# Gating an attention by a feed-forward network on one core: sums gathered earlier, q kept once in DRAM and read in two halves, some pieces moved between engines

## The chip, the core and the metric

The kernel runs on one core of a Trainium2 chip. The core has five engines that each follow their own instruction stream: TensorE (PE in the profile, its weight loads PEld), VectorE (DVE), ScalarE (ACT), GpSimd (POOL) and SyncE (SP), which here does nothing but issue DMAs. Each engine works through its stream in order and waits on semaphores for the others. DMAs are moved by 16 DMA engines that all queues share.

The metric is the device time of one execution in microseconds (us). The time before is the median of three runs; the profile is one execution of its own.

## The reference, cut to what matters

The input has 8 sequences of 512 positions and 256 features. Each is normalised, goes through an attention with 16 heads of 16 features (rotary positions, a causal window of 250) and, beside it, through three layers whose weights are plus or minus one; the second gates the first.

```python
xn = _layernorm(x)
proj = xn @ in_proj_w.T                      # q, k, v of 16 heads x 16
q, k = _apply_rope(q, k)                     # rotates the pairs of features
mask = (delta >= 0) & (delta < 250)          # delta = row - column
scores = where(mask, q @ k.T * 16 ** -0.5, lowest)
s = (softmax(scores) @ v) @ out_proj_w.T
h = relu(s0 * (concat(xn, -xn) @ sign(k0))) * 2    # 512 -> 1024
h = relu(s1 * (h @ sign(k1))) * 2                  # 1024 -> 1024
g = silu(s2 * (h @ sign(k2)))                      # 1024 -> 256
out = x + s * g
```

All arrays are float32 and the signs are booleans.

## The kernel before

**Number format.** [...] an operand is split into a high and a low part, and the products of the parts are added. For the scores this is done by stacking: a head has 8 pairs of features, and for each pair k is laid on partitions as high, low, high, low and q as high, low, low, high, so that one product over 64 partitions adds all four combinations. Two heads fill the 128 partitions of a tile. These *stacks* are made by going through DRAM: `to_dram` (L514) writes the split k and q of one sequence into a DRAM tile, each part twice, at the places that the order above asks for, and `stack` (L538) reads them back, 256 KB contiguous in DRAM to 128 partitions of 2 KB. A group g is four heads, so a group needs two stacks of k and two of q ("pair" 0 and 1), and a sequence has four groups.

**One sequence.** `prepare` normalises it in a transposed form. `stats` takes the moments on DVE, with a power on POOL (L278). `lay_down` (L302) writes them to DRAM, and `lay_over` (L311) reads them back as `of_all`, every partition getting all 512 means and factors. `norm_turned` applies them to `xT` on DVE (L322), and `sum_x` (L341, POOL) makes sums of its quarters, from which `project_seven` (L461) projects k and q with seven products in place of eight, for sequences 2 to 7; its counterpart sums of the weights are made once by `sum_weights` (L177 and L178, POOL). Sequence 1 uses `project` (L413). DVE multiplies the projections by the rotation's tables (L434, L498), `rotate` adds them up on POOL (L512), `split_hi` copies the high part on ACT (L528, tiles `kh` and `qh`, which share one buffer), and `split_lo` subtracts on DVE (L535, in place in `m_ka` and `m_qa`). Each split is followed by its writes to DRAM (L521).

**Attention.** The scores (L850) are taken in six steps of three blocks a sequence, two groups to three steps: groups 0 and 1 in steps 0 to 2, groups 2 and 3 in steps 3 to 5. ACT takes exponentials (L875), POOL masks them (L895, L902), and the products with v (L932) follow a step later. `v_columns` holds columns of ones, so the same product gives each row's sum. When a group is done, `keep` takes values V and sums S out of PSUM: for even groups on ACT (L956, L957), for odd ones on DVE (L950, L951). S has two buffers.

**Row sums.** For every two groups ("pair" of `divisions`), `gather` (L1022) writes four rows of each S to DRAM, `pack` (L1030) reads them back spread over 128 partitions, `invert` takes reciprocals on DVE (L1036) and writes them (L1038), `unpack` (L1049) reads them as rows, and `divide` spreads these over the partitions (L1055, DVE) and multiplies V (L1056, POOL).

**Gate.** `last` (L666) makes the third layer, `scale` (L704) takes it out of PSUM. `gate_ready` (L729) takes the exponential and adds one on ACT (L731, L732), takes two reciprocals of half a tile each on DVE (L737), and multiplies on POOL (L739). `project_o` (L1066) projects the attention, `product` and `store` multiply, add the residual (`xr`, L649) and write out (L1088, L1095, L1096).

**Order.** The order on every engine is written out by hand. Each piece of work has a planned time on PE's own scale, in which a sequence takes `SEQ = 42.0` (its feed-forward layers alone), and `run` sorts all pieces by it. A piece may return follow-ups with a delay against the clock of costs added so far. Only the order that results matters on the chip; the waits are by semaphores. `attention` places the six steps at the pieces' times nearest to equal shares of the work, and places the reads of the stacks. While sequence b goes through its layers, the next one's moments, projections and first stack are made, and the output of the one before is finished.

Of the kernel before, what the change touches and what calls it, by code (L numbers as in the profile page):

```python
# [11 lines left out]
F32 = mybir.dt.float32  # L12
# [4 lines left out]
ALU = mybir.AluOpType  # L17
# [17 lines left out]
def tile_attention_times_gated_ffn(  # L35
# [42 lines left out]
    nc = tc.nc  # L78
    P = 128
    B, T, E = x.shape  # L80
    H = HEADS
    D = E // H
# [38 lines left out]
    first_half, second_half = s_sb[:, 3:4], s_sb[:, 4:5]  # L121
# [112 lines left out]
    SEQ = 42.0  # L234
# [168 lines left out]
    def project(b, what, part, half=None):  # L403

        st = states[b]
        col = E * "qk".index(what) + P * "ab".index(part)
        if half == 1:
            ps = st.pop(part)
        else:
            ps = st[part] = bank(f"{what}{part}_ps_{b}")  # L410
        for cols in [slice(0, T)] if half is None else [ts(half, T // 2)]:
            for c in range(EC):
                nc.tensor.matmul(  # L413
                    ps[:, cols], wqkv_sb[:, c, ds(col, P)], st["xT"][:, c, cols],
                    start=(c == 0), stop=(c == EC - 1),
                )
        if half == 0:
            return

        m = turned.tile(  # L420
            [P, 2, T], F32, tag=f"m{part}", name=f"m_{what}{part}_{b}",
            bufs=2,
        )
        st[what, part] = m

        hi_after, lo_after = (4.0, 5.1) if b else (5.0, 6.2) if what == "k" else (4.6, 5.4)
        both_done = [
            (1.4, lambda: rotate(b, what)),
            (hi_after, lambda: split_hi(b, what)),
            (lo_after, lambda: split_lo(b, what)),  # L430
        ]

        def times(i):
            nc.vector.tensor_tensor(  # L434
                m[:, i], ps, rope_sb[:, i if part == "a" else 1 - i], ALU.mult
            )

        def both():
            times(0)
            times(1)  # L440
            if part == "b":
                return both_done

        return [(1.5 if b == 0 and what + part == "qb" else 0.0, both)]
# [69 lines left out]
    def to_dram(b, what, part, tile_):  # L514

        st = states[b]
        if part == 0:
            st["dram", what] = dram.tile([P, 8, T], F32, tag=what, name=f"d{what}_{b}")
        for turn in range(2):
            place = 2 * turn + (part ^ (turn if what == "q" else 0))  # L520
            nc.sync.dma_start(  # L521
                st["dram", what][:, ds(2 * place, 2), :], tile_.bitcast(F32)
            )

    def split_hi(b, what):
# [12 lines left out]
    def stack(b, g):  # L538
        st = states[b]
        for pair in range(2):  # L540
            for what in "kq":
                t = stacks.tile([P, T], F32R, tag=f"{what}{pair}", name=f"{what}_{b}_{g}_{pair}")
                rows = st["dram", what][ds(32 * g + 16 * pair, 16)]
                nc.sync.dma_start(t.bitcast(F32), rows.rearrange("p n t -> (p n) t"))  # L544
                st[what, g, pair] = t

    def prepare(b, plain=False):
# [205 lines left out]
    def late(b, u):  # L753

        if b + 1 == B:
            return last_at(b, 3) + L3 + 0.9 * u
        return SEQ * (b + 1) + (33.5 + 4.9 * u if b + 2 < B else 19.2 + 5.0 * u)

    def finish_ffn(b, u, how):
        quick.add(last_at(b, u))  # L760
        out = [(last_at(b, u), L3 * (2 if b + 1 < B else 1), lambda: last(b, u, how))]
        if how == "later":
            out += [
                (late(b, u) - (6.6 if b + 2 < B else 4.6), 0, lambda: gate_ready(b, u)),
                (late(b, u) - 4.2, 0, lambda: residual(b, u)),
            ]
        return out
# [175 lines left out]
    def keep(b, g, po):  # L943

        st = states[b]
        odd = g % 2
        S = st["S", g] = outs.tile([P, T], F32, tag="S", name=f"S_{b}_{g}", bufs=2)
        if odd:
            V = st["V", g // 2]
            nc.vector.scalar_tensor_tensor(V, po, second_half, V, ALU.mult, ALU.add)  # L950
            nc.vector.tensor_copy(S, po)  # L951
        else:
            V = st["V", g // 2] = outs.tile(
                [P, T], F32, tag=f"V{g // 2}", name=f"V_{b}_{g}", bufs=2
            )
            nc.scalar.mul(V, po, first_half)  # L956
            nc.scalar.copy(S, po)  # L957

    def flush():
        if pending:  # L960
# [12 lines left out]
    def attention(b, among):  # L973

        first, end = SEQ * b + (24.7 if b == 0 else 0.0), ends_at(b)
        inside = sorted((at, cost) for at, cost, _ in among if first <= at < end)
        whole = sum(cost for _, cost in inside)
        times, done = [], 0.0
        places = {}
        for at, cost in inside:  # L980
            if at in quick or b == 0 and at not in inner:
                places[at] = done
            done += cost
        for n in range(len(steps)):
            at = min(places, key=lambda at: abs(places[at] * len(steps) - whole * n))
            del places[at]
            times.append(at - 0.01)
        out = []
        for n in range(len(steps)):
            out.append((times[n], 2.5, lambda n=n: step(b, n)))  # L990
        for g in range(NG):

            at = times[used[g - 2][-1]] + 0.01 if g > 1 else first - (
                7.6 if b == 0 else 4.0 if b == 1 else 9.0
            )
            if b and g == 3:
                at += 5.0
            if b and g == 1:
                at = first + 0.01
            out.append((at, 0, lambda g=g: stack(b, g)))  # L1000
        if b + 1 == B:
            out.append((end, 0.7, flush))
        return out
# [105 lines left out]
    def divisions(b, pairs=(0, 1)):  # L1109
        out = []  # L1110
        for pair in pairs:
            if b + 1 < B:
                first = SEQ * b + (30.0 if b else 38.4) if pair == 0 else SEQ * (b + 1) + 3.0
            else:
                first = SEQ * b + (22.5 if pair == 0 else 33.4)
            pieces = (gather, pack, invert, unpack, divide)
            very_last = b + 1 == B and pair == 1
            for f, at in zip(
                pieces,
                (0.0, 2.0, 4.4, 6.4, 9.0) if very_last  # L1120
                else (0.0, 2.4, 5.2, 7.6, 14.0 if pair and b + 2 < B else 10.6),
            ):
                out.append((first + at, 0, lambda p=pair, f=f: f(b, p)))
        return out
# [17 lines left out]
    def swap():  # L1142
# [5 lines left out]
        (-34.6, 0, signs), (-40.5, 0, lambda: warm(9)), (-34.7, 0, lambda: warm(0)),  # L1148
        (-31.0, 0, lambda: enough(0)),
        (-32.7, 0, lambda: first_parts(2, 3)),  # L1150
        (19.2, 0, make_w2), (22.5, 0, swap), (27.0, 0, sum_weights), (SEQ * (B - 1) + 47.6, 0, add_up),
        (SEQ * (B - 1) + 44.0, 0, hint),
    ]
    for c in range(EC):
# [153 lines left out]
```

## Time and profile before

| | |
|---|---|
| median of 3 runs | 634.32 us (632.41 to 639.65) |
| the profiled execution, its time | 632.67 us |
| its span, first to last instruction | 630.9 us |
| busy: PE, PEld | 598.9, 387.4 us |
| busy: DVE, ACT, POOL | 364.7, 314.9, 306.4 us |
| mean granted clock of PE | 0.983 |
| DMA | 92.27 MB in all; HBM read 53.22 MB, written 38.30 MB |
| q stacks read (L544) | 64 DMAs of 256 KB |
| q written (L521) | 32 DMAs of 512 KB |

A line of the groups or of a timeline gives a start or a count, a busy time, the engine, the line of the kernel, the operation and "out<-in" with the shapes; what stands in brackets is the engine's idle time just before and the instruction that ended it. A line of waits reads: who waited, for whom, us in total, how many times, the longest. For SP the duration is that of the issue, not of the transfer. A row of windows gives, for a stretch of time, its length, the busy time of each engine with its number of instructions, the granted clock, the mean busy share of the 16 DMA engines, and the rate in GB/s.

### The profile page before, as it was taken

To read this page: it belongs to the slowest core of one execution; us is meant where nothing else is said; L and a number is where in the kernel's file an instruction comes from. 1 tells how busy PE (TensorE), PEld (TensorE's weight loads), DVE (VectorE), ACT (ScalarE), POOL (GpSimd) and SP (SyncE) were. 2 spreads that over 40 slices of the span, in tenths; PEclk is the share of its full clock that TensorE was granted. 3 is DMA by queue.
4 is the path that set the end of the run, shared out by engine and by line. 5 is a ranking of instruction groups with operands and counts; after the bars stand their busy time and mean duration, and the time that the engine had idled before them with its cause. 6 is when DMAs were issued, how large, how long until landed. Compare 5 with 4: busy or idle time off the path is not lost.

```text
span 630.9 us, 10724 instructions
## 1 busy us (share of the span) xinstructions
PE 598.9 (95%) x3860; PEld 387.4 (61%) x3860; DVE 364.7 (58%) x638; ACT 314.9 (50%) x607; POOL 306.4 (49%) x502
## 2 busy tenths in 40 slices
PE   7998989999799998999989998999989999899996
PEld 6653656675566655566555764656646675567785
DVE  6835415676446864559634686357943679335346
ACT  4646554544446554454545445364545546465521
POOL 2737532647426473265533664344744456445513
PEclk9998989999899998999989999899999999999999
DMA  8663754207633076331753218441364505632101
GB/s 273 264 220 119 262 157 130 102 1 286 216 107 102 27 264 216 104 102 68 274 166 103 101 77 296 136 134 69 132 256 144 179 2 222 220 101 86 53 25 54
DMA packets 50089, 92.27 MB, mean 146 GB/s; under 512 B 10992, under 2 KB 18672, under 8 KB 50032
## 3 DMA queue, kind: packets, MB, share of 16 engines
q1 hardware_dynamic: 47600, 89.31, 41.4%
q10 hardware_dynamic: 2432, 2.23, 1.2%
q8 instruction: 32, 0.52, 0.3%
q14 instruction: 25, 0.20, 0.1%
HBM read 53.22 MB, written 38.30 MB: 145 GB/s over the span
## 4 chain that ended last, share of the span: by engine, by line
PE 63%; DVE 13%; DMA 9%; SPq 4%; POOL 4%; ACT 3%; issue 3%; POOLq 0%; ACTq 0%; DVEq 0%
PE h_ps L614 28%; PE po L932 9%; PE z_ps L666 9%; PE sc L850 5%; DMA q<-dq 5%; PE v_ps L393 4%; DMA dsums<-S 3%; PE k_ps L461 3%; DVE m_qa L498 2%; SPq L521 2%; DVE den L737 2%; PE q_ps L461 1%; DVE m_qa L535 1%; SPq L544 1%; DVE m_kb L498 1%
## 5 line engine op out<-in xcount | busy, mean ns | idle before, releaser
L875 ACT ACTIVATE p<-sc 128x512 f32<-128x512 f32 (+2 forms) x288 | 150.7, 601 | 69.5 <-PE sc L850 46.4
L895 POOL TENSOR_SCALAR_AFFINE_SELECT p<-p 128x256 f32<-128x256 f32 (+1 forms) x224 | 103.1, 471 | 105.5 <-ACT p L875 83.3
L614 PE MATMUL h_ps<-h1l,w_sb 128*128 128x512 f32 (+1 forms) x576 | 143.4, 391 | 0.0
L614 PE MATMUL h_ps<-h1h,w_sb 128*128 128x512 f16 (+1 forms) x576 | 124.2, 359 | 0.0
L614 PEld LDWEIGHTS h_ps<-h1l,w_sb 128*128 128x128 f32 x576 | 101.0, 189 | 22.6 <-issue 0.3
L614 PEld LDWEIGHTS <-w_sb 128*128 128x128 f16 x704 | 61.5, 98 | 85.2 <-issue 39.9
L625 ACT ACTIVATE h2h<-h_ps 128x512 f16<-128x512 f32 (+1 forms) x72 | 39.7, 552 | 99.8 <-PE h_ps L614 99.8
L932 PE MATMUL po<-p,v_pad 128*32 128x378 f32 (+4 forms) x1152 | 78.3, 406 | 1.9 <-POOL p L902 1.9
L850 PE MATMUL sc<-q,k 64*128 64x378 f32 (+4 forms) x576 | 59.7, 318 | 20.8 <-DMA q<-dq 14.6
L623 DVE SCALAR_TENSOR_TENSOR h2l<-h_ps,h2h 128x512 fp32r<-128x512 f32 (+1 forms) x72 | 44.6, 620 | 52.0 <-ACT h2h L625 52.0
L850 PEld LDWEIGHTS sc<-q,k 64*128 64x128 f32 x576 | 45.7, 189 | 45.2 <-issue 19.5
L623 DVE SCALAR_TENSOR_TENSOR h1l<-h_ps,h1h 128x512 fp32r<-128x512 f32 x64 | 43.0, 686 | 44.6 <-ACT h1h L625 44.6
L902 POOL TENSOR_SCALAR_AFFINE_SELECT p<-p 128x256 f32<-128x256 f32 x144 | 63.1, 438 | 0.3 <-POOL p L895 0.3
L625 ACT ACTIVATE h1h<-h_ps 128x512 f16<-128x512 f32 x64 | 37.6, 602 | 32.5 <-PE h_ps L614 32.5
L614 PE MATMUL h_ps<-xl,w_sb 128*128 128x512 f32 x128 | 52.8, 493 | 0.0
L737 DVE RECIPROCAL den<-den 128x256 f32<-128x256 f32 (+1 forms) x32 | 51.6, 1629 | 0.8 <-ACT den L732 0.8
L1095 POOL TENSOR_TENSOR gate<-gate,xr 128x512 f32<-128x512 f32 (+1 forms) x15 | 18.7, 1248 | 64.2 <-DVE gate L1088 36.3
L932 PEld LDWEIGHTS po<-p,v_pad 128*32 128x32 f32 x1152 | 33.3, 116 | 26.4 <-issue 15.5
L512 POOL TENSOR_TENSOR m_ka<-m_ka,m_kb 128x512 f32<-128x512 f32 x16 | 24.4, 1545 | 49.1 <-DVE m_kb L498 39.5
L1056 POOL TENSOR_TENSOR V<-V,R 128x512 f32<-128x512 f32 x16 | 20.5, 1281 | 40.7 <-DVE R L1055 40.7
L614 PE MATMUL h_ps<-xh,w_sb 128*128 128x512 f16 x128 | 39.4, 390 | 0.0
L666 PE MATMUL z_ps<-h2l,w_sb 128*128 128x512 f32 (+1 forms) x144 | 35.7, 390 | 0.0
(144 smaller groups left out, 756.8 us busy)
## 6 DMA issues: line engine op xcount, KB each, us to landing
k<-dk SPq DMA_DIRECT2D x64, 256.0 KB
q<-dq SPq DMA_DIRECT2D x64, 256.0 KB
dk<-kh SPq DMA_DIRECT2D x16, 512.0 KB
dk<-m_ka SPq DMA_DIRECT2D x16, 512.0 KB
dq<-qh SPq DMA_DIRECT2D x16, 512.0 KB
dq<-m_qa SPq DMA_DIRECT2D x16, 512.0 KB
x<-in_x_dram SPq DMA_DIRECT2D x30, 128.0 KB
xT<-in_x_t_dram SPq DMA_DIRECT2D x7, 512.0 KB
```

Of the source, the lines that this page charges most:

```text
L393: nc.tensor.matmul(v.rearrange("p n s d -> p (n s d)"), st["xT"][:, c, ts(t, P)], wqkv_sb[:, c, 2 * E :], start=(c == 0), stop=(c == EC - 1),)
L461: nc.tensor.matmul(st["seven"][bank_][:, ts(half, H2)], a, b_, start=start and half == 0, stop=True, skip_group_check=True,)
L614: nc.tensor.matmul(ph, weights(w, p, c, ts(f, P)), st[src + p][:, c, cols], start=(k == 0), stop=(k == n - 1),)
L623: nc.vector.scalar_tensor_tensor(lo, ph, 0.0, hi, ALU.max, ALU.subtract)
L625: high = lambda: nc.scalar.activation(hi, ph, AF.Relu)
L666: nc.tensor.matmul(pz, weights(w2, p, c, ts(f, P)), st["h2" + p][:, c, cols], start=(c == 0 and p == "h"), stop=(c == NF1 - 1 and p == "l"),)
L737: nc.vector.reciprocal(part, part)
L850: nc.tensor.matmul(sc[r + (4 if y else 2 * pair)][:, ds(at, n)], st["k", g, pair][row, ts(j, P)], st["q", g, pair][row, ds(j * P + first, n)],
L875: nc.scalar.activation(p, s_, AF.Exp, scale=D ** -0.5)
L895: nc.gpsimd.affine_select(out=block, in_=block, compare_op=ALU.is_ge, fill=0.0, base=0, pattern=[[0, heads], [1, P]], channel_multiplier=-1,)
L902: nc.gpsimd.affine_select(out=block, in_=block, compare_op=ALU.is_ge, fill=0.0, base=-1, pattern=[[0, heads], [-1, beyond]], channel_multi ...
L932: nc.tensor.matmul(po[32 * r : 32 * r + 32, ds(j * P + first, n)], v_columns(j, g, r), place(tiles_, r, y, off, n), start=(j == 0), stop=( ...
```

## The change

Eight edits, on the work's order and on how q goes through DRAM:

- `gather` of the first pair of groups is moved ahead by 6.5 in the plan for all sequences but the last, while `pack` and what follows keep their places. On SP the gather then stands ahead of the writes of the next sequence's k and q (for sequence 0, between those of k and of q) and no longer behind them.
- q is written once per part instead of twice. The DRAM tile is laid out by head, copy, pair of features and part. A q stack is read by two DMAs, one per head, each taking 32 rows of DRAM and repeating them to 64 partitions: the source is a view of shape [2, 32, 512] with step 0 in its first dimension. k is still written twice and read as before; in its second copy the parts change places.
- `gate_ready` of the first output half moves from 6.6 to 19.8 ahead of the output projection, that of the second to 7.9, in all sequences but the last two. In the order that results, the first half's reciprocals stand ahead of the shuffle in `divide` of the second pair, and no longer between the rotation's products and the low part of k.
- `keep` of the even groups of sequence 0 goes from ACT to DVE.
- The first stack of sequence 0 stands ahead of `lay_down` of the moments on SP, the second one behind it; both stood behind it.
- `sum_weights` stands ahead of the first masks on POOL, and no longer between the masks of step 1.
- The high part of q of sequence 1 is copied 0.7 earlier in the plan, which puts it ahead of one `h2h` on ACT.
- With `inner.add`, the moved gather is not a place where a step of sequence 0 may be put. The order on PE stays as it was.

```diff
--- before.py
+++ after.py
@@ -424,6 +424,8 @@
         st[what, part] = m
 
         hi_after, lo_after = (4.0, 5.1) if b else (5.0, 6.2) if what == "k" else (4.6, 5.4)
+        if b == 1 and what == "q":
+            hi_after = 3.3
         both_done = [
             (1.4, lambda: rotate(b, what)),
             (hi_after, lambda: split_hi(b, what)),
@@ -515,11 +517,15 @@
 
         st = states[b]
         if part == 0:
-            st["dram", what] = dram.tile([P, 8, T], F32, tag=what, name=f"d{what}_{b}")
-        for turn in range(2):
-            place = 2 * turn + (part ^ (turn if what == "q" else 0))
+            n = 1 if what == "q" else 2
+            st["dram", what] = dram.tile(
+                [H, n, D // 2, 2, 2, T], F32, tag=what, name=f"d{what}_{b}"
+            )
+        d = st["dram", what]
+        for turn in range(d.shape[1]):
             nc.sync.dma_start(
-                st["dram", what][:, ds(2 * place, 2), :], tile_.bitcast(F32)
+                d[:, turn, :, part ^ turn].rearrange("h p i t -> h p (i t)"),
+                tile_.bitcast(F32).rearrange("p i t -> p (i t)"),
             )
 
     def split_hi(b, what):
@@ -540,8 +546,16 @@
         for pair in range(2):
             for what in "kq":
                 t = stacks.tile([P, T], F32R, tag=f"{what}{pair}", name=f"{what}_{b}_{g}_{pair}")
-                rows = st["dram", what][ds(32 * g + 16 * pair, 16)]
-                nc.sync.dma_start(t.bitcast(F32), rows.rearrange("p n t -> (p n) t"))
+                of_heads = st["dram", what][ds(4 * g + 2 * pair, 2)]
+                rows = of_heads.rearrange("h r p a i t -> (h r p a i) t")
+                if what == "k":
+                    nc.sync.dma_start(t.bitcast(F32), rows)
+                else:
+                    for r in range(2):
+                        nc.sync.dma_start(
+                            t[ts(r, 64)].bitcast(F32),
+                            rows[ts(r, 32)].unsqueeze(0).broadcast_to([2, 32, T]),
+                        )
                 st[what, g, pair] = t
 
     def prepare(b, plain=False):
@@ -761,7 +775,7 @@
         out = [(last_at(b, u), L3 * (2 if b + 1 < B else 1), lambda: last(b, u, how))]
         if how == "later":
             out += [
-                (late(b, u) - (6.6 if b + 2 < B else 4.6), 0, lambda: gate_ready(b, u)),
+                (late(b, u) - ((19.8, 7.9)[u] if b + 2 < B else 4.6), 0, lambda: gate_ready(b, u)),
                 (late(b, u) - 4.2, 0, lambda: residual(b, u)),
             ]
         return out
@@ -953,8 +967,12 @@
             V = st["V", g // 2] = outs.tile(
                 [P, T], F32, tag=f"V{g // 2}", name=f"V_{b}_{g}", bufs=2
             )
-            nc.scalar.mul(V, po, first_half)
-            nc.scalar.copy(S, po)
+            if b == 0:
+                nc.vector.tensor_scalar(V, po, first_half, None, ALU.mult)
+                nc.vector.tensor_copy(S, po)
+            else:
+                nc.scalar.mul(V, po, first_half)
+                nc.scalar.copy(S, po)
 
     def flush():
         if pending:
@@ -991,12 +1009,12 @@
         for g in range(NG):
 
             at = times[used[g - 2][-1]] + 0.01 if g > 1 else first - (
-                7.6 if b == 0 else 4.0 if b == 1 else 9.0
+                7.9 if b == 0 else 4.0 if b == 1 else 9.0
             )
             if b and g == 3:
                 at += 5.0
-            if b and g == 1:
-                at = first + 0.01
+            if g == 1:
+                at = first + 0.01 if b else at + 0.2
             out.append((at, 0, lambda g=g: stack(b, g)))
         if b + 1 == B:
             out.append((end, 0.7, flush))
@@ -1115,10 +1133,13 @@
                 first = SEQ * b + (22.5 if pair == 0 else 33.4)
             pieces = (gather, pack, invert, unpack, divide)
             very_last = b + 1 == B and pair == 1
+            early = 6.5 if b + 1 < B and pair == 0 else 0.0
+            if early:
+                inner.add(first - early)
             for f, at in zip(
                 pieces,
                 (0.0, 2.0, 4.4, 6.4, 9.0) if very_last
-                else (0.0, 2.4, 5.2, 7.6, 14.0 if pair and b + 2 < B else 10.6),
+                else (-early, 2.4, 5.2, 7.6, 14.0 if pair and b + 2 < B else 10.6),
             ):
                 out.append((first + at, 0, lambda p=pair, f=f: f(b, p)))
         return out
@@ -1148,7 +1169,7 @@
         (-34.6, 0, signs), (-40.5, 0, lambda: warm(9)), (-34.7, 0, lambda: warm(0)),
         (-31.0, 0, lambda: enough(0)),
         (-32.7, 0, lambda: first_parts(2, 3)),
-        (19.2, 0, make_w2), (22.5, 0, swap), (27.0, 0, sum_weights), (SEQ * (B - 1) + 47.6, 0, add_up),
+        (19.2, 0, make_w2), (22.5, 0, swap), (24.4, 0, sum_weights), (SEQ * (B - 1) + 47.6, 0, add_up),
         (SEQ * (B - 1) + 44.0, 0, hint),
     ]
     for c in range(EC):
```

## Prediction, made before the run

> **What bounds the kernel now.** I read the page first, then the waits, then the timelines of SyncE (SP, which issues nearly all DMAs in order), TensorE (PE) and VectorE (DVE) over one middle sequence, then windows of DMA rate.
>
> ```profile
> PE 598.9 (95%) x3860; PEld 387.4 (61%) x3860; DVE 364.7 (58%) x638; ACT 314.9 (50%) x607; POOL 306.4 (49%) x502
> ```
> PE is the bound: some 32 us of idle time are left in 630.9, and a clock of 0.983 costs at most another 10.7. The waits name most of the idle time, and one that is hidden so far:
>
> ```profile
> PE sc L850 <- DMA q<-dq: 14.6, 9, 2.6
> ...
> ACT S L957 <- DMA dsums<-S: 30.1, 7, 4.6
> ```
> Six times, once a sequence, PE waits for the first q stack of the next sequence. SP's timeline tells why:
>
> ```profile
> 141.36 0.80 SPq L521 DMA_DIRECT2D dk<-kh  x2
> ...
> 149.41 2.56 SPq L521 DMA_DIRECT2D dq<-m_qa  x2
> 152.01 2.46 SPq L1022 DMA_DIRECT2D dsums<-S  x2
> 156.99 0.32 SPq L1030 DMA_DIRECT2D sums<-dsums  x1
> ...
> 158.79 0.43 SPq L544 DMA_DIRECT2D q<-dq  x1
> ```
> The gather of the sums (L1022) queues behind 3 MB of k and q writes, and the stacks queue behind its landing. On PE:
>
> ```profile
> 161.10 0.59 PE L850 MATMUL sc<-q,k 64*128 64x378 f32 x4 [0.73 <-DMA q<-dq]
> 164.28 0.88 PE L850 MATMUL sc<-q,k 64*128 64x378 f32 x8 [2.58 <-DMA q<-dq]
> ```
> 3.3 us are lost here, and the granted clock of the window 160 to 170 is 0.83.
>
> A second chain has no slack, though PE does not wait on it: row inverses, then the moments of the next sequence (of_all), DVE, POOL, k projection.
>
> ```profile
> 184.66 0.32 SPq L1038 DMA_DIRECT2D inv<-sums  x1
> ...
> 191.32 1.06 SPq L1049 DMA_DIRECT2D rows<-inv  x2
> 192.54 0.35 SPq L311 DMA_DIRECT2D of_all<-d  x1
> ```
> ```profile
> 202.13 1.17 POOL L341 TENSOR_TENSOR xs<-xT 128x256 f32<-128x256 f32 x1
> ```
> ```profile
> 203.57 1.46 PE L461 MATMUL k_ps<-xs,w_sums 128*128 128x256 f32 x6
> ```
> The last POOL sum ends at 203.30, its product starts at 203.57. Whatever delays of_all delays PE one for one.
>
> **The change, part by part.** K is the start of a k projection: 125.6 and 203.3 in the chain; from 125.6 to 508.8 there are five periods, 76.6 us each.
>
> *Gather ahead of the writes.* Two issues (2.46) and the landing (to 156.99) leave the path from the last q write to the first stack. The gather now makes SP wait for the copy of S (about K+1), ahead of the kh write, at which SP sits until K+15.7 anyway: nothing needed sooner is behind it. ScalarE's (ACT's) 4.6 us waits for S go.
>
> *q written once.* 1 MB less: at the 413 GB/s of the window 150 to 155, 2.5 us of backlog. SP saves two issues a sequence.
>
> *Reciprocals.* The first pair stands in the chain now:
>
> ```profile
> 141.47 3.35 DVE L737 RECIPROCAL den<-den 128x256 f32<-128x256 f32 x2
> 144.74 1.16 DVE L535 TENSOR_TENSOR m_ka<-m_ka,kh 128x1024 fp32r<-128x1024 f32 x1
> ```
> Without it the low part of k starts 3.2 earlier, but qh reuses kh's buffer and waits for that write: its data ends at 144.9 now, 143.9 when ACT drops two den passes (1.25) ahead of kh. So qh gains 2.0, not 3.2 (145.98 to 144.0). The reciprocals go ahead of the shuffle of R, where DVE idles 3.42 for rows: free; uncovered they would cost 3.3. The ACT passes delay an h2h with 0.89 of idle time by 0.4, hidden by free PSUM banks. The second pair moves by one h2l, and POOL's product passes one add (1.28, on a store nobody waits for).
>
> *Start.* The four POOL sums (0.73 each) go from between masks, where PE waits 1.90 at 55.30, into 6.07 us of POOL idle time before 41.18: a gain of 1.9, and up to 1.7 of clock (0.83 from 50 to 60). Two ACT copies (0.70 and 0.58) go to DVE, idle for half of the window 56 to 76; qh of sequence 1 gains one h2h (0.6). The first stack no longer waits for the moments: from 34.8 to about 30.2. PE needed it at 39.44 and did not wait, so alone this gains nothing.
>
> *q read twice over.* A stack now issues six DMAs for four (at 0.43, 0.9 us more SP time). The bytes stay, the form does not: 128 KB with a leading step-0 dimension of 2 on the DRAM side, 64 rows on the other. No load of before has this form, so I bound it. **The near row** is the wide load:
>
> ```profile
> 197.00:198.50 1.50, 1.50 (x9) 0.95 (x9) 1.47 (x3) 0.05 (x1) 0.00 (x0) 1.00 1.03 396
> ```
> DMA share 1.03 at 396 GB/s: sixteen engines of some 24.5 GB/s. At that rate 128 KB take 0.33 us, a stack's 1 MB 2.7 as now. **The rule** speaks against it: the Trainium skill, "DMA: Bandwidth & Descriptors" (How many engines, in the section on why a DMA increments its semaphore by 16; again under rules for kernel authors), says that a copy spreads over the largest number up to 16 that divides both sides' slowest dimension, and that a leading zero-stride broadcast of c copies holds it to c engines. Here c is 2. The trace agrees as far as it goes: in its packet records a 512 KB write of 128 rows ends with 16 completion packets, the eight-row moments with 8, the four-row gathers with 4; of_all, broadcast too, has a leading 128 and ends with 16. By the rule 64 KB go through each of two engines: 2.7 us a DMA, and all four of a stack through the same lowest-numbered two, as the page says (no run here shows which). A stack is then 4 x 2.7 and 2 x 0.67 for k: **12.1 us for 2.7**. I take the rule; its near row, the small gathers, follows it.
>
> **The sum on two engines.** Every later DMA has its share on these two queued behind the q loads.
> - First stack: the last q write lands at 150.0 (K+24.4: qh at 144.0; 2.25 MB of writes at 413 GB/s). First bytes follow an issue by 1.0, then 11.4 and 0.4 to land: K+37.3, which is 162.9 against 164.1. PE's wait shrinks by only about 1.
> - Second: behind xr, a store and the inverse's round trip, issued at K+40.3, landed at K+54.5. PE came to step 1 at K+53.9, now about K+53: it waits 1.5.
> - Third: behind the x loads (1.6) and a gather that SP sits out (2.3); its q loads end at K+70.
> - The inverse, issued at about K+59, has its two engines' share behind them: landed K+70.4. Rows and moments follow; of_all is issued at K+71.9 (now K+66.9), done at K+75.7.
> - DVE, POOL, PE as now (6.6): next K at K+82.4. **+5.8 a period, +29 for five.** The two engines' own work checks it: 16 x 2.7 = 43, and some 25 for the rest (41.4% of 630.9 without today's q reads and dropped writes, an eighth of it): 68 of 82.
>
> Start: the last q write lands at 30.1, the first stack at 31.0 + 11.4 + 0.4 = 42.8 (PE there at 39.9), the second at 55 (PE step 1 at 47), xT and of_all behind it at 57.7; DVE's four passes of 0.7 let the first ka projection end at 61.8 instead of 49.8: +12, less the 1.9. Stack three then holds the two engines to 69.8, the kh write to 72.5, stack four to 84.7, the other k and q writes to 90.1; sequence 1's first stack lands at 102.8, and PE resumes there at 103 instead of 85.98. Step 1 follows at 119 (15.9 on, as now) and frees stack three's buffers: its q loads end at 131, of_all at 137.5, K is 144 instead of 125.6: **+18**. End: of the last sequence stack two lands at 508.8 + 54.5 = 563.3 (PE at 555.9), and stack four, behind a third sums' round trip, loses 3 more: **+10**.
>
> 632.67 (the profiled execution, 1.8 outside its span) + 18 + 29 + 10 = 689.7. The median shown is 1.65 above that execution; I forecast **690**.
>
> **Rivals.**
> *A: the reads spread over 16 engines (0.16, faster).* Then a stack's loads stay at 2.7; the first lands by K+29, PE is there at K+34, and of_all is not touched. The gain is 14.6 of q waits, 1.9 for POOL, 2.2 where PE waits for ACT behind S (at 85.98) and up to 10.3 of clock: 632.7 - 29.0 + 1.65 = 605. For it: the near row, and of_all. Against: its leading dimension is 128, not 2. The point from which it decides is four engines: a stack is then 6.7, lands at K+32.7, before PE, and clears the third stack's inverse early.
> *B: narrow, but only the start pays (0.13).* If of_all has slack that I don't see, the steady part gains 1 us six times and the start loses 18: 632.7 + 18 - 6 + 1.65 = 646. Against: 203.30 to 203.57.
> *C: all cancels (0.03)*, within 1% of 634, which is about what a measurement of this kernel tells from no change.
> The forecast has 0.68; its own range is 660 to 725 (packets 10% faster or slower: 4 us a period; half clock after longer PE waits on the upper side). With B and C the range is 632 to 725; A is left out. Faster 0.16, same 0.03, slower 0.81.
>
> **What would show it.** Right: q<-dq x128 of 128 KB, DMA share near 0.1 to 0.2 for stretches of 8 us and more after a stack's issue while few GB/s move; PE waits for q or k in steps 0 and 1, and for xs at the k projection; PE share under 90%; HBM written 8.4 MB less. ACT's wait for dsums and the reciprocals ahead of m_ka gone either way. Wrong: if stacks still land 3 us after their issue, step "two engines" fails and A holds.

## The result and the profile after

The kernel after takes **755.73 us** (median of four runs, 752.1 to 763.73) against 633.37 for the kernel before beside it: 1.194 times as long, interval [1.182, 1.206]. The direction was forecast, the size was not: 690 was forecast, and the range ended at 725.

Some executions of a kernel run at a lower clock and take over 1.5% longer, as the first profiled one of the kernel after did (clock 0.896, span 761.9): medians and ranges here are of all executions, ratios and their intervals leave these out. All lines and sums below come from a second execution of the same kernel (`after_again` among the experiments), with a span of 752.1 and a clock of 0.920. From its page, the busy times, the bytes and the form of the q reads:

```profile
PE 636.1 (85%) x3860; PEld 400.4 (53%) x3860; DVE 369.7 (49%) x642; ACT 313.9 (42%) x603; POOL 305.2 (41%) x502
...
HBM read 53.22 MB, written 29.91 MB: 111 GB/s over the span
...
q<-dq SPq DMA_DIRECT2D x128, 128.0 KB
```

PE runs the same 3860 products. It is idle for 116 us where it was idle for 32, and the products themselves take 37 us more: the same work at a clock of 0.920 and not 0.983. The 8.4 MB of writes are gone. Its waits, as in the view of before (who waited, for whom, us, times, longest):

```profile
DVE R L1073 <- DMA rows<-inv: 96.8, 12, 11.9
PE sc L864 <- DMA q<-dq: 83.2, 40, 3.4
...
ACT qh L534 <- DMA dk<-kh: 26.6, 7, 4.4
PEld sc L864 <- DMA q<-dq: 23.8, 12, 2.7
```

PE's wait for q has gone from 14.6 to 83.2, and VectorE waits 96.8 for the rows of the inverse, where it waited 54.0. ACT's wait for dsums is gone, but a new one has come: `qh` waits for the write of `kh` in seven sequences. SyncE's timeline over one period, which begins with the k projection at 153.1 (K):

```profile
177.57 0.66 SPq L526 DMA_DIRECT2D dq<-m_qa  x1
...
183.08 1.16 SPq L555 DMA_DIRECT2D q<-dq  x2
...
189.36 0.57 SPq L1056 DMA_DIRECT2D inv<-sums  x1
199.57 1.07 SPq L1067 DMA_DIRECT2D rows<-inv  x2
...
201.66 1.10 SPq L555 DMA_DIRECT2D q<-dq  x2
...
218.68 1.12 SPq L555 DMA_DIRECT2D q<-dq  x2
...
235.45 0.35 SPq L311 DMA_DIRECT2D of_all<-d  x1
```

A q stack goes out every 17 to 19 us. SP issues the 16 KB of inverses at 189.36, behind the first stack, but the rows that need them only at 199.57, and the second stack stands behind these rows. The packet records show why: of the 128 packets of the inverse (128 bytes each), 112 go out by 191.6, and the other sixteen, which is two engines' share of 128 rows, only between 198.3 and 199.0, when the q reads end. On PE, step 0 of the next sequence and then the next k projection:

```profile
192.02 0.47 PE L864 MATMUL sc<-q,k 64*128 64x378 f32 x3 [2.33 <-DMA q<-dq]
195.53 0.65 PE L864 MATMUL sc<-q,k 64*128 64x378 f32 x1 [3.04 <-DMA q<-dq]
198.21 1.29 PE L864 MATMUL sc<-q,k 64*128 64x378 f32 x7 [2.03 <-DMA q<-dq]
```
```profile
245.43 1.79 PE L463 MATMUL k_ps<-xs,w_sums 128*128 128x256 f32 x4 [1.41 <-POOL xs L341]
```

The waits end 3.5 and 2.7 us apart, each with one more 128 KB read of q: 2.7 us is what the forecast gave to a 128 KB DMA on two engines. In the windows (length, then busy time of PE, PEld, DVE, ACT and POOL, granted clock, DMA share, GB/s), ahead of that stall's main part and in it:

```profile
185.00:191.00 6.00, 4.69 (x19) 2.47 (x17) 1.79 (x3) 0.60 (x1) 1.86 (x5) 1.00 0.48 141
191.50:197.50 6.00, 1.11 (x4) 0.58 (x4) 0.00 (x0) 1.08 (x2) 0.00 (x0) 0.75 0.14 49
```

From 191.6 to the end of the window all data moves in packets of 2 KB, at 49 GB/s. Two engines of sixteen are a DMA share of 0.125; the view shows 0.14. The half clock outlasts the stall: 0.50 from 198 to 200 and 0.65 from 200 to 202, when PE is busy again.

### The profile page after: what moved, and what is told of

The parts are those of the page before. It is cut to its first block, busy times and chain, and to the rows that moved or that the text cites. A ratio compares the mean times of both kernels' runs of the same rounds, so it can differ in the third digit from the quotient of the medians.

```text
span 761.9 us, 10788 instructions
## 1 busy us (share of the span) xinstructions
PE 648.6 (85%) x3860; PEld 407.9 (54%) x3860; DVE 369.7 (49%) x642; ACT 314.3 (41%) x603; POOL 304.9 (40%) x502
## 5 line engine op out<-in xcount | busy, mean ns | idle before, releaser
L909 POOL TENSOR_SCALAR_AFFINE_SELECT p<-p 128x256 f32<-128x256 f32 (+1 forms) x224 | 96.4, 441 | 170.8 <-ACT p L889 137.0
L864 PE MATMUL sc<-q,k 64*128 64x378 f32 (+4 forms) x576 | 76.0, 346 | 89.0 <-DMA q<-dq 83.0
L628 PE MATMUL h_ps<-h1l,w_sb 128*128 128x512 f32 (+1 forms) x576 | 147.6, 399 | 0.0
L628 PE MATMUL h_ps<-h1h,w_sb 128*128 128x512 f16 (+1 forms) x576 | 126.0, 362 | 0.0
L864 PEld LDWEIGHTS sc<-q,k 64*128 64x128 f32 x576 | 54.4, 206 | 119.9 <-issue 80.5
L628 PEld LDWEIGHTS h_ps<-h1l,w_sb 128*128 128x128 f32 x576 | 103.8, 194 | 23.7 <-issue 0.3
L946 PE MATMUL po<-p,v_pad 128*32 128x378 f32 (+4 forms) x1152 | 93.7, 473 | 0.0
L946 PEld LDWEIGHTS po<-p,v_pad 128*32 128x32 f32 x1152 | 38.3, 132 | 32.0 <-issue 25.2
L628 PE MATMUL h_ps<-xl,w_sb 128*128 128x512 f32 x128 | 54.9, 510 | 0.0
L628 PE MATMUL h_ps<-xh,w_sb 128*128 128x512 f16 x128 | 41.7, 410 | 0.0
```

What stands on the lines that cost most here:

```text
L628: nc.tensor.matmul(ph, weights(w, p, c, ts(f, P)), st[src + p][:, c, cols], start=(k == 0), stop=(k == n - 1),)
L864: nc.tensor.matmul(sc[r + (4 if y else 2 * pair)][:, ds(at, n)], st["k", g, pair][row, ts(j, P)], st["q", g, pair][row, ds(j * P + first, n)],
L909: nc.gpsimd.affine_select(out=block, in_=block, compare_op=ALU.is_ge, fill=0.0, base=0, pattern=[[0, heads], [1, P]], channel_multiplier=-1,)
L946: nc.tensor.matmul(po[32 * r : 32 * r + 32, ds(j * P + first, n)], v_columns(j, g, r), place(tiles_, r, y, off, n), start=(j == 0), stop=( ...
```

## The experiments

Three readings were open. **Two engines**: the step-0 view holds a read to two engines. **Repeated rows**: reading rows twice costs by itself. **The order**: the moves do the harm. Each batch of runs has its own runs of the kernel before (medians 626.8, 633.0, 633.1 and 631.9), so kernels are compared by their ratio to it. "Period" is the mean of the five stretches from K to K.

### Is it the form of the q reads?

`edits_only` is the kernel after with `to_dram` and `stack` of the kernel before:

```diff
-                [H, n, D // 2, 2, 2, T], F32, tag=what, name=f"d{what}_{b}"
+            st["dram", what] = dram.tile([P, 8, T], F32, tag=what, name=f"d{what}_{b}")
...
+                rows = st["dram", what][ds(32 * g + 16 * pair, 16)]
+                nc.sync.dma_start(t.bitcast(F32), rows.rearrange("p n t -> (p n) t"))
```

> All the moves of order of the change, with the DRAM layout, the double write of q and the wide stack reads of before. Theory 1 (the two-engine reads make the loss): the waits of PE for q stacks, for POOL's masks and for ACT behind S go, 600 to 612 us, and the period from one k projection to the next falls from 76.6 to 71 to 73. Theory 2 (repeating the same rows in one read is what is slow, whatever the engines): the same here. Theory 3 (the moves of order do the harm): 700 us or more.

Measured: 596.48, ratio 0.951 [0.946, 0.956], period 71.9. PE has hardly anything left to wait for between the first and the last k projection:

```profile
115.70:475.00 359.30, 358.07 (x2302) 228.02 (x2302) 234.38 (x391) 191.51 (x371) 190.81 (x306) 1.00 0.45 156
```

The moves of order alone are a gain of 4.9%, at a clock of 1.00. So the reading "the order" falls. This is also the fastest kernel of this study.

`q_once_wide` is the kernel after with the same bytes read twice over, in another form:

```diff
-                    for r in range(2):
-                        nc.sync.dma_start(
-                            t[ts(r, 64)].bitcast(F32),
-                            rows[ts(r, 32)].unsqueeze(0).broadcast_to([2, 32, T]),
-                        )
+                    for r in range(4):
+                        nc.sync.dma_start(t[ts(r, 32)].bitcast(F32), rows[ts(r // 2, 32)])
```

> The changed kernel, but each q stack is read by four DMAs of 32 rows in place of two with a leading step-0 dimension of 2; q is still once in DRAM and its rows are still read twice. Theory 1: 16 engines carry each read, 605 to 618 us (ten issues a stack instead of six cost SP 1.8 us a stack, which PE sees only in part). Theory 2: rows are still read twice, from the same addresses, so 690 us or more. Theory 3: 700 or more.

Measured: 601.77, ratio 0.959 [0.955, 0.964], period 71.9. Every row of q is still read twice, yet PE's 83 us of waits for q and 154 us of time are gone: "repeated rows" falls too. Against `edits_only` only the start is longer (K at 120.3 and not at 115.7); no gain from writing q once is left to see, though its reads here also take eight issues a stack and not two.

### How many engines?

In `q_once_2` and `q_once_4` the 32 rows of a head lie in DRAM in 2 or 4 runs with two rows of padding behind each, so that a read of 32 rows has a leading dimension of 2 or 4, without any step 0. The lines of `q_once_2`:

```diff
+            shape = [H, n, D // 2, 2, 2, T] if what == "k" else [H, 2, 16 + 2, T]
...
+                    for r in range(4):
+                        nc.sync.dma_start(
+                            t[ts(r, 32)].bitcast(F32), of_heads[r // 2, :, : 16]
+                        )
```

> As the four-read kernel, but q's rows in DRAM are padded so that a read has a leading dimension of 2 (groups of 16 rows) and no step 0. Theory 1: two engines carry each read, q<-dq shows a DMA share of 0.13 while it drains, and the time is that of the changed kernel within 2%, 740 to 770 us. Theory 2: no row is repeated within a read, so it is as fast as the wide reads.

> As the four-read kernel, but q's rows in DRAM are padded so that a read has a leading dimension of 4 (groups of 8 rows) and no step 0. Theory 1: four engines carry each read, a stack of q takes 5.4 us of them; the prediction's turning point says faster than before, 610 to 632 us. Theory 2: as fast as the wide reads, within 3 us. Theory 3: 700 or more.

Measured: 744.27, ratio 1.186 [1.177, 1.196], for two, and 643.4, ratio 1.026 [1.018, 1.033], for four. Two leading rows without step 0 are as slow as the kernel after, and stall in the same way; a window of `q_once_2`:

```profile
196.00:200.00 4.00, 0.65 (x1) 0.31 (x2) 0.00 (x0) 0.00 (x0) 0.00 (x0) 0.50 0.13 49
```

Four was still slower than the kernel before (each of the two was run only twice). To see from where on the count stops to matter, `q_once_8` and `q_once_16` are made in the same way (runs of 4 and of 2 rows).

> As q_once_4, but q's rows lie in DRAM in eight runs of four rows, with two rows of padding behind each run, so that a 32-row read has a leading dimension of 8. If the count of engines decides, a read of 64 KB goes over eight engines in 0.33 us, a stack's q loads take about 1.4 in place of 2.7 on four engines: first stack some 3 earlier than in q_once_4, ahead of PE, and the time is near q_once_wide's: 602 to 612. If what costs is that the rows are not contiguous in DRAM (more descriptors a read), it stays near q_once_4's 643.

Measured: 630.86, ratio 1.003 [0.996, 1.009], period 74.5: neither 602 to 612 nor 643. So a cost was left that `q_once_wide` doesn't have.

> As q_once_8, with runs of two rows and two rows of padding behind each, so that a 32-row read has a leading dimension of 16. q_once_8 took 631 and not 602 to 612. If its 29 us over q_once_wide come from the padded form (an issue of such a read keeps SP 0.70 us, that of a contiguous 32-row read 0.43), this one takes about the same, 625 to 632. If they come from having eight engines and not sixteen, it takes 600 to 608.

Measured: 618.8, ratio 0.983 [0.976, 0.990], period 72.7: between the two expectations. The form itself costs something with all sixteen engines at hand, and the tile view shows one difference. SP's issues of the q reads (duration in ns, min/median/max) in `q_once_wide`, `q_once_16` and `q_once_8`:

```profile
L555 SPq DMA_DIRECT2D q<-dq x256: 302/420/1587, 31.2 to 540.1; - x128
```
```profile
L562 SPq DMA_DIRECT2D q<-dq x256: 543/590/1567, 33.0 to 559.2; - x128
```
```profile
L562 SPq DMA_DIRECT2D q<-dq x256: 650/657/1556, 31.2 to 571.4; - x128
```

An issue of a read in runs keeps SP for 0.59 to 0.66 us (0.61 for four, 0.60 for two), that of a contiguous one for 0.42. That the longer issues make the difference was not tried alone (the writes of q have another form too); of the 17 us between `q_once_16` and `q_once_wide`, only 4 lie in the five periods.

The four padded kernels have nearly the same issue time, so they can be set in a row: periods of 72.7 with sixteen leading rows, 74.5 with eight, 76.3 with four, **90.8 with two**. Each of the first halvings costs 1.8 us a period, the last one 14.5. PE waits for q 8.8, 17.0, 21.4 and 71.9 us in all. With sixteen to four, only the stretch from step 0 to step 1 grows (14.6, 16.4 and 18.1 us against 13.8 in `q_once_wide`): the first stack alone is late. With two, the second stack and the k projection are late as well.

The packet records also count the engines. A DMA ends with packets of 4 bytes, sixteen for a 512 KB write of 128 rows. The padded kernels and `q_once_wide` all have 256 q reads and differ in nothing else that counts here, and they have 8337 such packets with sixteen leading rows (and in `q_once_wide`), 6289 with eight, 5265 with four and 4753 with two. That is 4241 plus 256 times 16, 8, 4 and 2. The kernel after has 128 q reads and 4497, which is 4241 plus 128 times 2.

### Do the moves matter once the reads are narrow?

`narrow_only` is the kernel before with `to_dram` and `stack` of the kernel after, and nothing else of the change:

```diff
-            st["dram", what] = dram.tile([P, 8, T], F32, tag=what, name=f"d{what}_{b}")
+                [H, n, D // 2, 2, 2, T], F32, tag=what, name=f"d{what}_{b}"
...
+                            rows[ts(r, 32)].unsqueeze(0).broadcast_to([2, 32, T]),
```

> The kernel before with nothing changed but q: written once, read by two DMAs with step 0 in all groups; all moves of order left out. If the two engines' queue sets the period whatever stands around it, the moves' gain of 30 us is swallowed and this takes what the kernel after takes, 750 to 770. If narrow reads and the order add up, it takes 627 + 159 = 785. If the moves do harm once the reads are narrow (the first pair's gather ahead of the writes, the first stack ahead of the moments), it takes less than the kernel after: 720 to 745.

Measured: 778.01, ratio 1.230 [1.217, 1.243], period 93.4. It lies between the first two expectations. Against 1.196 for the kernel after, the moves still gain some 3%, less than the 4.9% that they gain by themselves. They do no harm.

### Which group's reads cost what?

In `narrow_group_0` to `narrow_group_3` only one group of each sequence is read by the narrow form, the others as in `q_once_wide` (here for the first group, g = 0):

```diff
+                    if g == 0:
                         for r in range(2):
...
+                    else:
+                        for r in range(4):
+                            nc.sync.dma_start(t[ts(r, 32)].bitcast(F32), rows[ts(r // 2, 32)])
```

> The kernel after, but only the first group's q stack of each sequence is read by the narrow form (two DMAs with step 0); the other three groups by four DMAs of 32 rows, as in q_once_wide (601.8, period 71.8). Theory Q, PE's stall at the first stack is the larger part: the first read is issued at K+28, lands 13 to 15 later at K+41 to K+43, PE is there at K+34.4 and has no idle time elsewhere to give, so the period is 78 to 80 and the time 645 to 660. Theory P, the one of the prediction (the period is set by the inverse and of_all behind the third group's reads, the first stack costs about 1 us a period): 601 to 612. Theory E, any narrow group costs a quarter of what all four cost over wide reads: 602 + 38 = 640.

> The kernel after, but only the third group's q stack is read by the narrow form. Theory Q: PE comes to step 3, the first that uses it, at K+67; the read is issued at K+49.4 and lands by K+64, so PE does not wait; the rows of the inverse and of_all (issued K+61.2) are held a few us at most: 602 to 615, period 72 to 73.5. Theory P: of_all is held by 5 or more in each period and the k projection with it, period 77 or more: 635 to 645. Theory E: 640.

> The kernel after, but only the second group's q stack is read by the narrow form. Periods measured so far: 71.8 with no narrow group, 82.0 with the first alone (+10.2), 77.4 with the third alone (+5.6), 92.2 with all four (+20.4). If the groups' losses add up, the second and the fourth together cost about 4.6. The second's reads are issued at K+38.7 and land by K+53; PE's step 1 is at K+48.2, so this one costs 4 to 6 and its period is 76 to 77.5, 630 to 645. If they overlap (a late first stack delays the issue of the second as well), the second alone costs as much as the first, 80 to 82.

> The kernel after, but only the fourth group's q stack is read by the narrow form. It is issued at K+62, just behind of_all (K+61.2), and its first user, step 4, is at K+83: neither PE nor the moments should wait for it, so the period stays within 71.8 to 73 and the time at 601 to 612. If any 10 us on the two engines hold up something (the residual's loads, the row inverses), it is 77 or more, 640.

| narrow group | time | ratio, interval | period | over 71.9 |
|---|---|---|---|---|
| first | 679.35 | 1.076 [1.065, 1.087] | 81.9 | +10.0 |
| second | 655.36 | 1.040 [1.032, 1.048] | 78.8 | +6.9 |
| third | 640.01 | 1.011 [1.000, 1.022] | 77.5 | +5.5 |
| fourth | 611.34 | 0.972 [0.965, 0.979] | 72.1 | +0.2 |
| all (kernel after) | 754.19 | 1.196 [1.189, 1.202] | 90.7 | +18.8 |

The first is dearer than expected, the second too; the fourth is free in the periods (its start is longer, K at 127.1 for 120.3), and the four together (22.6) come to a little more than all at once. The costs sit in different places. With the first group narrow, PE's timeline shows the stall at step 0 and a k projection without any wait:

```profile
174.08 0.68 PE L868 MATMUL sc<-q,k 64*128 64x378 f32 x3 [1.57 <-DMA q<-dq]
177.42 0.65 PE L868 MATMUL sc<-q,k 64*128 64x378 f32 x1 [2.66 <-DMA q<-dq]
180.09 1.29 PE L868 MATMUL sc<-q,k 64*128 64x378 f32 x7 [2.03 <-DMA q<-dq]
...
219.68 1.46 PE L463 MATMUL k_ps<-xs,w_sums 128*128 128x256 f32 x6
```

With the third group narrow it is the other way round, step 0 runs through and the k projection waits:

```profile
172.46 1.07 PE L868 MATMUL sc<-q,k 64*128 64x378 f32 x12
...
198.09 0.70 PE L463 MATMUL k_ps<-xT,wqkv_sb 128*128 128x256 f32 x2 [1.72 <-DVE h2l L641]
...
200.63 1.13 PE L463 MATMUL k_ps<-xs,w_sums 128*128 128x256 f32 x4 [1.40 <-POOL xs L341]
```
```profile
188.12 1.08 SPq L1071 DMA_DIRECT2D rows<-inv  x2
190.03 0.34 SPq L311 DMA_DIRECT2D of_all<-d  x1
```

Here of_all goes out 68.9 after its K (121.1), where in `q_once_wide` it does so at 61.2 (181.5 after 120.3). About half of PE's stall comes by a way that the forecast did not name: PE waits for `h2l`, a piece of the feed-forward layers that stands on VectorE behind the rows and of_all and so is late with them. Both theories hold, each for a group of its own: the forecast's chain through the inverse and the moments for the third, PE's stall for the first and the second.

### Why is the first stack so late?

In the kernel after, `qh` waits for the write of `kh`:

```profile
175.05 1.05 ACT L534 CAST qh<-m_qa 128x1024 fp32r<-128x1024 f32 x1 [4.02 <-DMA dk<-kh]
```

The new DRAM layout puts the two copies of a head side by side, so that a write's first dimension on the DRAM side is 16 heads and not 128 rows. In the packet records the mean of a 4 KB packet (nearly nine in ten of them writes of k and q) is 172 ns before and 198 after. `k_copies_outer` puts the copies outermost:

```diff
-                [H, n, D // 2, 2, 2, T], F32, tag=what, name=f"d{what}_{b}"
+                [n, H, D // 2, 2, 2, T], F32, tag=what, name=f"d{what}_{b}"
...
-                d[:, turn, :, part ^ turn].rearrange("h p i t -> h p (i t)"),
+                d[turn, :, :, part ^ turn].rearrange("h p i t -> (h p) (i t)"),
...
-                    nc.sync.dma_start(t.bitcast(F32), rows)
+                    for r in range(4):
+                        nc.sync.dma_start(
+                            t[ts(r, 32)].bitcast(F32), rows[r % 2, ts(r // 2, 32)]
+                        )
```

> The kernel after with q as narrow as there, but the copies outermost in DRAM, so that each write of k and q addresses 128 rows in its first dimension on the DRAM side (16 heads in the kernel after), as in the kernel before; k stacks are then read by four DMAs of 32 rows each. If the longer writes come from the 16-row form, a write's packets take 160 ns and not 200 to 400, qh waits less for the kh write, and the last q write's landing follows its issue by 3 in place of 5.4: the first stack lands 3 to 4 earlier, and as PE stalls for it one for one, the period is 88 to 89.5 and the time 725 to 738. If the writes' form doesn't matter, or the six more issues a stack (0.43 each) eat it, it stays at 750 to 760.

Measured: 764.53, ratio 1.213 [1.206, 1.220]. That is no gain, though the waits of `qh` for the kh write had shrunk to 0.6 us in its profile. The six added issues were the suspect, so they were then tried alone, in three kernels on one chip; `k_in_four` keeps the layout of the kernel after:

```diff
-                    nc.sync.dma_start(t.bitcast(F32), rows)
+                    for r in range(4):
+                        nc.sync.dma_start(t[ts(r, 32)].bitcast(F32), rows[ts(r, 32)])
```

> The kernel after, unchanged, as the measure for the two beside it: 750 to 760, periods of 90 to 92.

> The kernel after, but each k stack tile is read by four DMAs of 32 rows instead of one of 128; the layout in DRAM and its longer writes stay. If SP's issues are on the path (six more a stack at 0.43, of which those of the first k tile are hidden behind the wait for the q write, so 1.3 to 2.6 a stack), the period grows by 3 to 6 over the kernel after and the time is 775 to 800; the slow writes then cost what lies between this and k_copies_outer (764), 10 to 35. If the issues are free, because the two engines are still busy with the stack before, it takes the same as the kernel after, 750 to 760, and the longer k writes cost nothing in the end.

> k_copies_outer once more beside the other two: 760 to 768, 5 to 10 above the kernel after.

Measured: 754.19, 778.89 and 761.94; ratios 1.196 [1.189, 1.202], 1.232 [1.224, 1.240] and 1.206 [1.200, 1.213]. The tile view of `dk`, for `k_in_four` and then for `k_outer_again`: SP's issues of the kh writes with their durations.

```profile
L526 SPq DMA_DIRECT2D dk<-kh x16: 567/580/1557, 19.3 to 648.2; - x16
...
  ACT qh L534: 27.0, 7
```
```profile
L526 SPq DMA_DIRECT2D dk<-kh x16: 330/384/1703, 20.7 to 637.9; - x16
```

So splitting the k reads costs 25 us, most likely by its six issues more a stack (a cost of the smaller reads themselves was not tried apart), and taking the 16-head form of the writes away gives 17 of them back: the packets' mean falls to 175 ns, the issue of a write from 0.58 to 0.38 us, and ACT's wait from 27.0 to 3.6. **With narrow reads, the slower writes cost some 17 us; with wide ones nothing can be seen of them**: `q_once_wide` has the same writes, and a wait of `qh` of 22.1, at the same period as `edits_only`. The 17 us were measured beside the split k reads; without these they may be somewhat different.

## Why the forecast was right and wrong

**The rule of two engines was right, and rightly taken over the near row.** Stretches at 49 GB/s and a DMA share of 0.14, reads that come in 2.7 us apart, and `q_once_2`, which has two leading rows without a step 0, show it. The count of closing packets gives two for each read, and sixteen of the inverse's 128 packets wait for the q reads. That four or eight engines lie in between shows that the count decides. Which two engines carry the reads, no run shows.

**What was expected either way was right**: 8.4 MB less written, 128 reads of 128 KB, PE's share under 90% (85), ACT's wait for dsums gone.

**The sum was too small by half.** Against the profile of before:

| term | forecast | measured |
|---|---|---|
| start, first k projection (125.5 before) | +18 | +27.6 (153.1) |
| five periods (76.6 before) | +29 | +70.3 (90.7 each) |
| end, behind the last k projection | +10 | +23.3 |
| sum | +57 | +121.2 |

The periods hold 41 of the 64 us missed. Where PE loses them is read from the score products' times, averaged over sequences 2 to 6; a step's length is from its first product's start to its last one's end:

| stretch of the period | before | after | change | forecast |
|---|---|---|---|---|
| step 0 and up to step 1 | 3.9 + 13.8 | 9.8 + 14.4 | +6.5 | about -1 |
| step 1 and up to step 2 | 1.1 + 8.7 | 3.7 + 9.8 | +3.7 | +1.5 |
| step 3 and up to step 4 (k projection) | 1.1 + 15.3 | 2.3 + 18.6 | +4.5 | the rest, +5.3 |

*of_all.* The step on which the forecast rested holds: "next K at K+82.4" was wrong, but the share of it that the inverse and the moments cause was 5.3 and is 4.5, and the third group alone costs 5.5. Only about half of PE's stall there is the wait for xs that was forecast; the rest is for `h2l`, which VectorE reaches late.

*First stack.* "Lands at K+37.3 ... PE's wait shrinks by only about 1" is **the step that failed**: it lands at about K+45, and PE's loss grows. The first q read was to go out at K+24.4, when the last q write lands; in the mean of six periods it goes out at K+30.2. Two terms of the sum make these 5.8:

- `qh` starts at K+22.3, for K+18.5 in the forecast (144.0). In `edits_only`, with the old layout, it starts at K+18.9, as forecast; with the new layout and wide reads (`q_once_wide`) at K+20.2; the rest comes with the narrow reads. The forecast had seen that `qh` waits for the kh write, but took the write's duration from the old layout: it priced the q side of the new layout and treated k as unchanged.
- From the start of `qh` to the first q read 5.9 were allowed, and it takes 7.9. `q_once_wide` takes 7.8, so this was too short whatever the form of the reads.

From the first read's issue to the last landing it then takes about 15 where 12.9 had been summed; what makes these 2 us was not tried. How much the slow writes are worth shows in `k_outer_again` beside `k_in_four`: without them the first read goes out 1.9 earlier (K+28.1 for K+30.0), and step 0 is 1.8 shorter (8.0 for 9.8).

*Second stack.* Issued at K+48.8 and not K+40.3, used up to K+64.6 and not landed by K+54.5: the late first stack handed on, with the inverse queued behind its reads as forecast.

*Start and end.* The same terms once more. At the start, the first stack's reads go out at 30.8, near the forecast's 30.2, but the first stack of sequence 1 does so at 96.5, where its forecast landing (102.8) had it at about 90; step 0 ends at 113 for 103. At the end, stalls in steps 0, 1 and 2 of the last sequence add 23.3, where only stacks two and four had been counted.

*Clock.* The sum counted landings at full speed and left "half clock after longer PE waits" to the upper side of the range. PE's busy time grew by 37 us for the same instructions. Part of that is already in the table's gaps (14.4 for 12.7 without stalls, between steps 0 and 1); it belonged into the central sum. Not every stall brings it, though: from step 3 to step 4, with the k projection's stalls in it, `narrow_group_2` keeps a clock of 1.00 in three of five periods.

**The rivals.** A was priced well for a kernel that didn't come about: 605 forecast, which is 0.954 of before, and 0.959 in `q_once_wide`. Its turning point, four engines, was set too low: `q_once_4` is 2.6% slower than before. But that kernel also carries the padded form, which costs 2.4% at sixteen engines (0.983 for 0.959), so by this estimate the true point is not far from four. B ("only the start pays") falls with the periods of 90.7.

## What to carry to other kernels

When a transfer is held to a few engines, count for each consumer in turn how late it comes, the first one ahead of all: here the first stack alone cost 10.0 us a period, and the chain that had been studied 5.5. When one side of a shared layout changes, price the writes and reads of the other side in the new shape as well. Splitting a narrow read into contiguous 32-row pieces, each with a long leading dimension, removed the loss. The SP issues that it adds cost nothing in the periods of `q_once_wide` (71.9, as in `edits_only`); with SP on the path, splitting the k reads in the same way cost 25 us.

## What the runs showed of the hardware that was not expected

- A 512 KB write of 128 partitions took longer when its DRAM side led with 16 heads at a stride than with 128 rows: mean 4 KB packet 198 against 172 to 175 ns, SP's issue 0.58 against 0.38 us. Kernels of both forms have the same number of closing packets (7569 in `k_outer_again` and `k_in_four`), so it is not that fewer engines carry them. Why the packets are slower was not tried.
- SP's issue time depends on the read's form: 0.42 us for 64 KB in 32 contiguous rows, 0.59 to 0.66 for the same rows in padded runs. The kernels are at 0.959 and, with all sixteen engines, 0.983 of before; how much of this is the issues was not tried.
- The small round trips pay for the large reads: it took ten us (189.36 to 199.57) from the issue of 16 KB of inverses to that of the rows behind them, because an eighth of their packets lay behind a narrow stack.
- PE's granted clock falls in the stalls (0.75 and 0.50 in the windows shown) and stays low for some us behind them (0.50 and 0.65 from 198 to 202), against 1.00 over the whole middle of `edits_only`.
